# Layer 3's residual sums made by accumulating DMA stores instead of pool engine additions

## The chip, the cores and the metric

The kernel runs on one core of one Trainium2 chip. A core has five engines that run their own instruction streams and wait for each other by semaphores: TensorE (PE, matmuls into PSUM), VectorE (DVE), ScalarE (ACT), the pool engine (GpSimd, POOL) and SyncE (SP), which issues most of the transfers. Transfers run on 16 DMA engines that all issuers share; ScalarE and the pool engine issue some as well. The metric is the device time of the one launch in microseconds (us), as a median of runs.

## What is computed

The reference passes 2048 tokens (2 sequences of 1024) of 256 channels through four layers. Each layer makes a condition `c` from the stream `x` and adds a mixture of experts of that condition to the stream:

```
x = x + _L0_ffn_ref(_L0_cond_ref(x, ...), ...)
x = x + _L1_ffn_ref(_L1_cond_ref(x, ...), ...)
x = x + _L2_ffn_ref(_L2_cond_ref(x, ...), ...)
x = x + _L3_ffn_ref(_L3_cond_ref(x, ...), ...)
```

Layer 3 is where the change lies. Its condition is a shared two-matrix network plus two of eight experts for every token, weighted and divided by 3. Its last part, `_L3_ffn_ref`, sends each token to one of 16 experts, the one with the largest logit. An expert takes at most 160 tokens (the kernel plans 128 rows and 32 more for each), and what it writes for a token *replaces* that token's row:

```
safe_idx = jnp.where(valid, idx, bt)
y_flat = x_flat.at[safe_idx.reshape(-1)].set(out.reshape(-1, d), mode='drop')
```

Here `x_flat` is the condition itself. So the output of a token is `x + c` when it was not taken by an expert, and `x + out` when it was. With `x` the stream ahead of layer 3 and `c` its condition, every row of the output first needs the base value `x + c`, and the rows of taken tokens are then written over.

## The kernel before, in words

The work is tiled by 128 tokens: 16 tiles, in four blocks (`NB`) of 512 tokens (`TB`). The stream lies in the tile `Xt` (token-major, 128 partitions by 16 tiles by 256 channels); the condition of layer 3 is summed in `Ht`, which the profile calls `ACC`, as it lies in that buffer. `HT` and `XT` hold the channel-major copies that matmuls need.

**Layer 3's condition** (`_cond_moe`, called with `next` set to an object of class `Last`). A first phase does the shared network for blocks 0 to 2 (`lead` is 3). After each step of it a hook is called, and the hook advances the routing in the object `Lead`, whose counter `n` counts the calls: four for each block. The routing ends in 32 indirect scatters of `Xt` rows from the pool engine (L282). Then come the experts' slots, 37 of them in most cases: a load of rows, matmuls, and an indirect scatter of the results into the DRAM buffer `tbuf`. Then `next.begin()` prepares the last layer, and a second phase does the shared network for block 3 (`_shared`, matmuls at L1534 and L1520) and, in hooks, the tokens' sums.

**The sums** are in class `Tokens`. For each of the 16 tiles, SP loads the two expert results of each token (`yt`, L298, 256 KB, five buffers), and VectorE adds them with their weights into `ACC` (two instructions at L1665). A tile that is done is turned by TensorE (`ps_bk`, L1588) and copied by ScalarE into `HT` (L1591). Which tiles are due at which hook is a list (`by`).

**The last layer's routing** (`Last.chunk`) is cut into parts for each block of 512 tokens, and these are threaded into the hooks by a written-out plan: first `logits`, then `top`, `rows` and the `beats` that rank the tokens. `logits` is the part that the change edits. It issues from ScalarE a store of the block's condition rows into the left half of a DRAM buffer `hx` (L2217), and on the pool engine an addition of the block's condition into the stream, in place (L2219). Then come matmuls for the logits (`l3f_pt`, L2223). `top` has the small VectorE instructions on `l3f_pl` (L2236 to L2248, with an exponential on ScalarE at L2242); `rows` makes `l3f_z` and TensorE's `l3f_ps` (L2266), and on the pool engine a running count `l3f_cum` (L2271).

**`hx`** holds for each token its condition (left) and the stream ahead of layer 3 (right, one store of the whole `Xt` at L2190 in `begin`). The last layer gathers rows of it by expert (`Last.run`, L338 from the pool engine), computes, adds the right half to the result (L2427), and scatters the sums into the output (L2428, pool engine).

**The base rows** go to the output in `Last.finish`: four stores of 512 KB from SP (L2340), one for each block of `Xt`, after the pool additions. Behind them on SP stand the loads of the biases (`XT<-in_L_b`, L2345; `ACC<-in_L_b`, L2393) and of weights. The scatters into the output wait for these stores by name (`self.outs`).

**Order.** The program is recorded in Python; a scheduler places the instructions on the engines by what is ready, and `_behind` adds an order without a semaphore. A DMA has one of eight completion semaphores for its kind of issuer, in turn; a DMA that takes a semaphore over waits for the one that had it.

Of the kernel before, what the change touches and what calls it, by code (L numbers as in the profile page):

```python
# [15 lines left out]
ALU = mybir.AluOpType  # L16
# [4 lines left out]
P = 128  # L21
D = 256
# [5 lines left out]
TB = 512  # L28
NB = N // TB
# [1459 lines left out]
def _behind(k, inst, ref):  # L1489

    k.tc.add_manual_dep(inst.ins, ref.ins.name,
                        mybir.DependencyInfo(mybir.DependencyClass.NoSync,
                                             mybir.DependencyReason.SCHED_ONLY))
# [433 lines left out]
def _cond_moe(k, name, wr, bias, W1, W3, W2, nf, hold, R1, R2, gate_mult, final, lead, most, next=None):  # L1927

    nc, A, XT, HT, Xt, Ht = k.nc, k.A, k.XT, k.HT, k.Xt, k.Ht
    rp, pool, psum = k.rp, k.pool, k.psum  # L1930
    E, T, NS = 8, P, 39
    base = 0 if next else 8192
    w, rb = k.small[wr], k.small[bias]
    sets = []
    for i in range(4):
        r = k.ring.take(1, hold).rearrange("p (n c f) -> p n c f", n=2, f=D)
        sets.append([(r[:, 0], A[R1]), (r[:, 1], A[R2])])
    def routing(lead_):
        s = rp.tile([P, NT, E], F32, name=name + "_s", tag="s")
        _logits(k, psum, rp, XT, w, E, name, s, AF.Sigmoid, k.small[wr, "b"])  # L1940
        sel = rp.tile([P, NT, E], F32, name=name + "_sel", tag="lg")
        nc.vector.tensor_tensor(sel, s, _bc(rb, 1, [P, NT, E]), ALU.add)
        _, ixf = _top(nc, rp, sel, E, name)
        _name_rows(k, k.Xr, ixf, base)
        oh = [_one_hot(k, rp, ixf, n, E, name + "_oh%d" % n, "oh%d" % n) for n in range(2)]
        M = rp.tile([P, NT, E], F32, name=name + "_M", tag="M")
        nc.vector.tensor_add(M, oh[0], oh[1])
        cum = _running(k, rp, M, E, name)
        yield
        pos, eid, of, used = _route(k, rp, psum, M, cum, E, T, NS, len(sets), name)  # L1950
        rows = [_rows_of(k, rp, oh[n], pos, E, name + "_rows%d" % n, "rows%d" % n) for n in range(2)]
        k.x.begin()
        lead_.sends = k.x.paced(k.Xr, rows)

        nc.vector.tensor_mul(M, M, s)
        den = rp.tile([P, NT], F32, name=name + "_den", tag="den")
        nc.vector.tensor_reduce(den, M, AX.X, ALU.add)
        big = rp.tile([P, NT], F32, name=name + "_big", tag="big")
        nc.vector.tensor_single_scalar(big, den, 1e-9, ALU.is_gt)
        nc.vector.tensor_scalar_add(den, den, 1e-9)  # L1960
        nc.vector.reciprocal(den, den)
        nc.vector.tensor_mul(den, den, big)
        nc.vector.tensor_scalar(big, big, -0.5, 0.5, ALU.mult, ALU.add)
        gate = []
        for n in range(2):
            nc.vector.tensor_mul(oh[n], oh[n], s)
            g = rp.tile([P, NT], F32, name=name + "_g%d" % n, tag="g%d" % n)
            nc.vector.tensor_reduce(g, oh[n], AX.X, ALU.add)
            nc.vector.tensor_mul(g, g, den)
            nc.vector.tensor_add(g, g, big)  # L1970
            nc.vector.tensor_scalar_mul(g, g, gate_mult * final)
            gate.append(g)
        lead_.made = gate, eid, of, used

    def shared(tb, hook=None, mid=None, added=lambda: False):
        if nf == 8 and tb == 0:
            po = _shared_first(k, pool, psum, XT, W1, W3, W2, hook)
        else:
            po = _shared(k, pool, psum, XT, tb, W1, W3, W2, nf, hook, mid)
        for i in range(2):  # L1980
            t = tb * 4 + i * 2
            if added():
                nc.vector.scalar_tensor_tensor(Ht[:, t:t + 2, :], po[i], final, Ht[:, t:t + 2, :],
                                               ALU.mult, ALU.add)
            else:
                nc.scalar.activation(Ht[:, t:t + 2, :], po[i], AF.Copy, scale=final)

    lead_ = Lead(k, routing, *((1, 7), 2) if nf == 8 else ((1, 3), 4))
    def hook(f, mul, mm):
        if k.late and lead_.n >= 6:  # L1990
            k.late.pop(0)(mul)
        lead_.hook(f, mul, mm)

    for tb in range(lead):
        shared(tb, hook)
    gate, eid, of, used = lead_.finish()
    k.t.begin()
    by = Slots(k, pool, psum, of, base)

    def slots(lo, hi):  # L2000
        series = Series(k, by, lo, hi)
        for i in range(lo, hi):
            series.slot(i, _gelu_products(k, pool, psum), lambda: _slot_weights(k, eid, i, sets, E))
        series.close()

    used = nc.values_load(used[0:1, 0:1], min_val=0, max_val=NS)
    slots(0, most)
    with k.tc.If(used > most):  # L2008
        slots(most, NS)
    if next:  # L2010
        next.begin()
    c = Tokens(k, pool, psum, gate, Ht, HT, nf, next)
    for tb in range(lead, NB):
        c.there = tb * 4
        shared(tb, c.hook, c.hook, lambda: c.added >= tb * 4 + 4)
    c.there = NT
    k.ring.drop(hold)
    if next:
        next.finish(c)
    else:  # L2020
        c.finish()
# [104 lines left out]
class Last:  # L2126
# [46 lines left out]
    def begin(self):  # L2173

        k, nc = self.k, self.k.nc
        nc.vector.memset(self.acc, 0.0)
        for t in range(NT):
            c = sum((q + 1) * TB - max(t * P, q * TB) for q in range(t // 4, NB) if self.on_act(t))
            c -= P * sum(self.on_act(u) for u in range(4 * (t // 4) + 4) if u <= t)
            nc.gpsimd.memset(self.acc[:, t, 4:5], float(c))  # L2180
        nc.vector.memset(self.z, 0.0)
        for side, at, v in ((0, self.E, 1.0), (1, self.E, -1.0)):
            nc.vector.memset(self.z[:, :, side, at:at + 1], v)
        for i in range(3):
            nc.vector.memset(self.z[:, :, 0, self.PARTS + 2 * i:self.PARTS + 2 * i + 1], 1.0)
            nc.vector.memset(self.z[:, :, 1, self.PARTS + 2 * i + 1:self.PARTS + 2 * i + 2], -1.0)
        nc.vector.memset(self.cum[:, 0, :], 0.0)
        nc.vector.tensor_scalar(self.down, k.iota[:, 0:self.E], -1.0, float(self.E), ALU.mult, ALU.add)
        nc.vector.tensor_scalar_add(self.th, k.iota[:, 0:NT], 1.0)
        nc.sync.dma_start(k.hx[:, D:2 * D].rearrange("(t p) d -> p t d", p=P), k.Xt)  # L2190
        self.weights()

    def on_act(self, t):

# [11 lines left out]
    def chunk(self, q):  # L2206
        k, nc, E = self.k, self.k.nc, self.E
        pool, psum = k.pool, k.psum
        ts, cols = slice(4 * q, 4 * q + 4), slice(q * TB, (q + 1) * TB)
# [5 lines left out]

        def logits(mul, mm):
            nc.scalar.dma_start(k.hx[cols, 0:D].rearrange("(t p) d -> p t d", p=P), k.Ht[:, ts, :])  # L2217
            x = k.Xt[:, ts, :]
            nc.gpsimd.tensor_tensor(x, x, k.Ht[:, ts, :], ALU.add)  # L2219
            ps = psum.tile([P, P], F32, name="l3f_pt", tag="mm")  # L2220
            for c in range(2):
                for j in range(4):
                    i = nc.tensor.matmul(ps[32 * j:32 * j + 32, :], k.small["L3_Wg"][:, c, :],  # L2223
                                         k.HT[:, c, (4 * q + j) * P:(4 * q + j + 1) * P],
                                         start=c == 0, stop=c == 1, skip_group_check=True)
                    behind(i, mm)
            lt = got["lt"] = pool.tile([P, P], F32, name="l3f_lt")
            nc.scalar.copy(lt, ps)
# [94 lines left out]
    def finish(self, c):  # L2323

        k, nc, E = self.k, self.k.nc, self.E
# [4 lines left out]
        ref = None  # L2330
        for x in todo:
            if callable(x):
                x()
            else:
                for p in x:
                    ref = p(None, None) or ref
        ref = _warm(k, k.psum, ref, 6)
        assert c.put == NT
        for q in range(NB):
            i = nc.sync.dma_start(k.out[q * TB:(q + 1) * TB, :].rearrange("(t p) d -> p t d", p=P),  # L2340
                                  k.Xt[:, 4 * q:4 * q + 4, :])
            _behind(k, i, c.load)
            self.outs.append(i.ins.name)
        for e in range(E):
            i = nc.sync.dma_start(self.b2[:, e, :], k.A["L3_b2"][e:e + 1].to_broadcast([P, D]))  # L2345
            _behind(k, i, c.load)
# [7 lines left out]
        for h in range(4):  # L2354
            A = k.HT[:, 0, 256 * h:256 * h + 256].bitcast(BF16).rearrange("p (t r) -> p t r", r=P)
            ts = slice(4 * h, 4 * h + 4)
            made = nc.vector.tensor_tensor(A, _bc(k.iota16[:, 0:P], 1, [P, 4, P]),  # L2357
                                           _bc(rank16[:, ts], 2, [P, 4, P]), ALU.is_equal)
            for j in range(4):
# [3 lines left out]
                ref = i  # L2363
# [6 lines left out]
        ref = _warm(k, k.psum, ref, 4)  # L2370
        ps = k.psum.tile([P, 2, E], F32, name="l3f_pi2", tag="t", bufs=2)
        for t in range(NT):
# [3 lines left out]
            ref = i  # L2376
# [3 lines left out]
        for g in range(4):  # L2380
# [3 lines left out]
            ref = i  # L2384
        self.ref = ref
        s, d, _ = self.numbers(pg, 4, "g")
# [236 lines left out]
```

## Time and profile before

| what | us |
|---|---|
| median of 3 runs | 1445.5 (1445.5 to 1446.88) |
| the profiled execution | 1446.02 |
| its span, first to last instruction | 1444.3 |
| TensorE busy | 1396.8 (97% of the span) |
| VectorE busy | 464.0 (32%) |
| ScalarE busy | 307.8 (21%) |
| pool engine busy | 291.5 (20%) |
| the four additions at L2219 | 9.7, 2.418 each |

The granted TensorE clock is 0.988 on the mean. A row of a timeline gives the start in us, the duration, the engine, the line, the operation, what it writes and reads, the number of instructions merged into the row, and in brackets how long the engine sat idle ahead of it and what ended that. A row of a group or of a tile's list gives the count and the least, median and greatest duration in ns, and when the first and the last started. A row of busy time by stretch gives the stretch, its length, the busy time of PE, of the weight loads (PEld), DVE, ACT and POOL with the number of instructions, then the granted clock, the mean share in which the 16 DMA engines were busy, and GB/s.

### The profile page before, as it was taken

How to read it: one execution, taken by the hardware profiler on the slowest of the kernel's cores; microseconds unless marked ns; L12 is line 12 of the kernel's file. 1: busy time of each engine (PE TensorE's matmuls, PEld its weight loads, DVE VectorE, ACT ScalarE, POOL GpSimd, SP SyncE). 2: the span in 40 equal slices, each digit the busy share in tenths (PEclk: the TensorE clock that was granted, in tenths of full speed). 3: DMA queues.
4: the chain of work that ended last, by engine and by line, in shares of the span. 5: the costliest groups of instructions: out<-in, count | busy, mean ns of one | idle time of the engine just before them, and what ended most of it. 6: DMA issues, size and time to landing. Idle time of an engine off the chain costs nothing. (4 is left out here: it accounts for less than half of the span.)

```text
span 1444.3 us, 23566 instructions
## 1 busy us (share of the span) xinstructions
PE 1396.8 (97%) x8606; PEld 1002.0 (69%) x8610; DVE 464.0 (32%) x1558; ACT 307.8 (21%) x646; POOL 291.5 (20%) x339
## 2 busy tenths in 40 slices
PE   9999999999999999999999999999999998997897
PEld 4544444545558865565999999999995567874675
DVE  4523322326214442511211111111115513467332
ACT  3222221234112121201111111111112211126221
POOL 0400001200533410331001001001010073433441
PEclk9999999999999999999999999999999999998999
DMA  9879994922314850421335155155507247758470
GB/s 313 297 256 347 358 321 134 275 72 101 125 52 118 260 183 8 188 82 37 113 109 194 48 180 195 46 178 194 193 20 273 93 164 244 225 172 284 123 243 15
DMA packets 176527, 246.78 MB, mean 171 GB/s; under 512 B 16695, under 2 KB 128831, under 8 KB 176400
## 3 DMA queue, kind: packets, MB, share of 16 engines
q1 hardware_dynamic: 154912, 203.18, 43.1%
q0 software_dynamic: 13888, 36.63, 7.2%
q10 hardware_dynamic: 7600, 5.34, 1.1%
q8 instruction: 72, 1.18, 0.3%
q14 instruction: 55, 0.45, 0.1%
HBM read 280.92 MB, written 47.22 MB: 227 GB/s over the span
## 5 line engine op out<-in xcount | busy, mean ns | idle before, releaser
L282 POOL DMA_INDIRECT tbuf<-ys,sdst x108 | 106.3, 984 | 484.8 <-ACT ys L1844 376.6
L1520 PE MATMUL spo<-ring,sa 128*128 128x256 f32 x704 | 164.9, 379 | 0.0
L1520 PEld LDWEIGHTS spo<-ring,sa 128*128 128x128 f32 x704 | 132.5, 190 | 44.6 <-issue 29.1
L1837 DVE TENSOR_TENSOR fa<-fsg,fpu 128x512 f32<-128x512 f32 x72 | 49.5, 688 | 316.2 <-PE fpu L1832 316.2
L1832 PE MATMUL fpg<-xsT,ring 128*128 128x128 f32 x1152 | 140.4, 275 | 0.7 <-issue 0.7
L1543 DVE TENSOR_TENSOR sa<-ssg,spu 128x512 f32<-128x512 f32 x88 | 60.4, 686 | 249.8 <-PE spu L1534 241.2
L1832 PE MATMUL fpu<-xsT,ring 128*128 128x128 f32 x1152 | 140.4, 275 | 0.0
L1832 PEld LDWEIGHTS fpg<-xsT,ring 128*128 128x128 f32 x1152 | 137.0, 192 | 2.7 <-issue 0.9
L1832 PEld LDWEIGHTS fpu<-xsT,ring 128*128 128x128 f32 x1152 | 134.4, 192 | 0.0
L1841 PE MATMUL fpo<-ring,fa 128*128 128x256 f32 x576 | 130.3, 379 | 0.0
L1841 PEld LDWEIGHTS fpo<-ring,fa 128*128 128x128 f32 x576 | 106.7, 190 | 13.0
L1539 ACT ACTIVATE ssg<-spg 128x512 f32<-128x512 f32 x88 | 52.6, 597 | 263.0 <-PE spg L1534 243.6
L1534 PE MATMUL spg<-HT,ring 128*128 128x512 f32 x192 | 92.1, 594 | 2.2 <-issue 1.9
L1534 PE MATMUL spu<-HT,ring 128*128 128x512 f32 x192 | 90.2, 592 | 0.0
L1808 PE MATMUL cph<-xsT,ring 128*128 128x128 f32 x576 | 79.0, 281 | 4.8 <-DMA ring<-in_L_r 2.6
L1836 ACT ACTIVATE fsg<-fpg 128x512 f32<-128x512 f32 x72 | 43.0, 597 | 171.7 <-PE fpg L1832 171.7
L1808 PEld LDWEIGHTS cph<-xsT,ring 128*128 128x128 f32 x576 | 71.2, 194 | 8.8 <-DVE sn L1735 2.8
L1534 PE MATMUL spg<-XT,ring 128*128 128x512 f32 x160 | 75.5, 593 | 1.3 <-PEq L2008 1.2
L1534 PE MATMUL spu<-XT,ring 128*128 128x512 f32 x160 | 75.2, 592 | 0.0
L1815 PE MATMUL cpo<-ring,ch 128*128 128x256 f32 x288 | 73.8, 380 | 0.0
L1534 PEld LDWEIGHTS spu<-HT,ring 128*128 128x128 f32 x192 | 36.3, 190 | 45.0 <-issue 44.2
L1731 DVE COPY xsT<-ps_cm 128x256 f32<-128x256 f32 x132 | 55.1, 418 | 36.7 <-PE ps_cm L365 36.5
(621 smaller groups left out, 1726.1 us busy)
## 6 DMA issues: line engine op xcount, KB each, us to landing
ring<-in_L_w SPq DMA_DIRECT2D x108, 1024.0 KB
ring<-in_L_r SPq DMA_DIRECT2D x72, 512.0 KB
ring<-in_L_r SPq DMA_DIRECT2D x144, 256.0 KB
xs<-xbuf SPq DMA_DIRECT2D x132, 129.0 KB
ring<-in_L_W SPq DMA_DIRECT2D x32, 512.0 KB
yt<-tbuf SPq DMA_DIRECT2D x48, 256.0 KB
XT<-in_L_r SPq DMA_DIRECT2D x16, 512.0 KB
HT<-in_L_r SPq DMA_DIRECT2D x8, 512.0 KB
```

Source lines behind the costliest of these rows:

```text
L282: i = k.nc.gpsimd.indirect_dma_start(out=self.ap, out_offset=bass.IndirectOffsetOnAxis(ap=idx, axis=0), in_=rows, in_offset=None, **end)
L1520: mm = nc.tensor.matmul(po[g // 2][:, g % 2, :], a[:, g * P:(g + 1) * P], W2[:, f, :], start=f == 0 and g % 2 == 0, stop=f == nf - 1, skip ...
L1534: mm = nc.tensor.matmul(ps, W[:, c, f * P:(f + 1) * P], X[:, c, cols], start=c == 0, stop=c == 1)
L1539: k.silu = nc.scalar.activation(sg, pg, AF.Silu)
L1543: mul = nc.vector.tensor_mul(a, sg, pu)
L1731: turned = nc.vector.tensor_copy(xT, _channel_major(k, self.psum, xs, made=made))
L1808: made = [nc.tensor.matmul(ph[:, f, :], R1[:, c, f * P:(f + 1) * P], xT[:, c, :], start=c == 0, stop=c == 1) for f in range(2) for c in ra ...
L1815: made = [nc.tensor.matmul(po, h[:, f, :], R2[:, f, :], start=f == 0, stop=f == 1) for f in range(2)]
L1832: made = [nc.tensor.matmul(ps[:, j, :], W[:, c, (f0 + j) * P:(f0 + j + 1) * P], xT[:, c, :], start=c == 0, stop=c == 1) for ps, W in ((pg, ...
L1836: nc.scalar.activation(sg, pg, AF.Silu)
L1837: nc.vector.tensor_mul(a[:, f0:f0 + 4, :], sg, pu)
L1841: made = [nc.tensor.matmul(po, a[:, f, :], W2[:, f, :], start=f == 0, stop=f == 4 * nh - 1) for f in range(4 * nh)]
```

## The change

The store of the whole `Xt` to the right half of `hx` moves out of `begin` into a new method `base`, which also stores `Xt` to the output. `base` is called from the hook of the first phase, at the fourth call. In `logits` the pool engine's addition is replaced by a DMA that the pool engine issues, which adds the block's condition rows onto the rows in the output. The four stores of finished sums in `finish` go. So `Xt` keeps the stream ahead of layer 3 to the end.

```diff
@@ _cond_moe, hook
         lead_.hook(f, mul, mm)
+        if next and lead_.n == 4:
+            next.base(mul)
@@ Last.begin
-        nc.sync.dma_start(k.hx[:, D:2 * D].rearrange("(t p) d -> p t d", p=P), k.Xt)
         self.weights()
+
+    def base(self, ref):
+
+        for to in (self.k.hx[:, D:2 * D], self.k.out):
+            i = self.k.nc.sync.dma_start(to.rearrange("(t p) d -> p t d", p=P), self.k.Xt)
+            if ref is not None:
+                _behind(self.k, i, ref)
@@ Last.chunk, logits
-            x = k.Xt[:, ts, :]
-            nc.gpsimd.tensor_tensor(x, x, k.Ht[:, ts, :], ALU.add)
+            i = nc.gpsimd.dma_start(k.out[cols, :].rearrange("(t p) d -> p t d", p=P), k.Ht[:, ts, :],
+                                    accum_op=ALU.add)
+            self.outs.append(i.ins.name)
@@ Last.finish
-        for q in range(NB):
-            i = nc.sync.dma_start(k.out[q * TB:(q + 1) * TB, :].rearrange("(t p) d -> p t d", p=P),
-                                  k.Xt[:, 4 * q:4 * q + 4, :])
-            _behind(k, i, c.load)
-            self.outs.append(i.ins.name)
```

## The prediction

> **What bounds the kernel now.** I read the page's busy shares first: TensorE is busy 97% of the span, so most of the kernel can't be touched by an edit on the pool engine. I then went to the chain that ended last, in order of time, and looked where it leaves TensorE. From 1283 to 1343 us it runs over VectorE (the adds of layer 3's condition into `ACC`, then the routing of the last layer). So I read this stretch engine by engine. The pool engine's timeline there has the four additions that the change removes:
>
> ```profile
> 1288.46 2.48 POOL L2219 TENSOR_TENSOR Xt<-Xt,ACC 128x1024 f32<-128x1024 f32 x1 [8.40 <-issue]
> 1294.34 2.48 POOL L2219 TENSOR_TENSOR Xt<-Xt,ACC 128x1024 f32<-128x1024 f32 x1 [3.40 <-DVE ACC L1665]
> 1300.22 2.35 POOL L2219 TENSOR_TENSOR Xt<-Xt,ACC 128x1024 f32<-128x1024 f32 x1 [3.40 <-DVE l3f_m L2236]
> ...
> 1309.32 2.36 POOL L2219 TENSOR_TENSOR Xt<-Xt,ACC 128x1024 f32<-128x1024 f32 x1 [3.90 <-DVE l3f_lg L2238]
> ```
>
> Beside them, VectorE's instructions on the tile `yt`, and its timeline:
>
> ```profile
> L1665 DVE SCALAR_TENSOR_TENSOR ACC<-yt,l3c_g,ACC x32: 470/474/2596, 1284.0 to 1308.7; 128x256 f32<-128x256 f32 x32
> ```
>
> ```profile
> 1286.43 5.59 DVE L1665 SCALAR_TENSOR_TENSOR ACC<-yt,l3c_g,ACC 128x256 f32<-128x256 f32 x8
> 1291.94 0.68 DVE L1543 TENSOR_TENSOR sa<-ssg,spu 128x512 f32<-128x512 f32 x1
> 1292.54 5.36 DVE L1665 SCALAR_TENSOR_TENSOR ACC<-yt,l3c_g,ACC 128x256 f32<-128x256 f32 x8
> ...
> 1300.25 0.23 DVE L2238 TENSOR_TENSOR l3f_lg<-l3f_pl,l3f_m 128x64 f32<-128x64 f32 x1
> 1300.51 2.12 DVE L2241 TENSOR_SCALAR l3f_eq<-l3f_lg 128x64 f32<-128x64 f32 x1
> 1302.66 0.22 DVE L2243 TENSOR_TENSOR l3f_eq<-l3f_eq,l3f_down 128x64 f32<-128x64 f32 x1
> ```
>
> An add at L1665 takes 474 ns, but two take about 2590, and those two start inside the first two pool additions and end as they end. The third addition catches `l3f_eq`: 2.12 us, where the same instruction takes 0.19 at 1312.28. So each of three additions stops VectorE: 2.12 + 2.11 + 1.93 = 6.2 us. The fourth falls into a VectorE wait for TensorE (2.37 us, to 1311.66).
>
> Is that on the path? TensorE's timeline answers:
>
> ```profile
> 1298.46 0.60 PE L1588 MATMUL ps_bk<-ident,ACC 128*128 128x128 f32 x4
> 1298.90 0.27 PE L2232 MATMUL l3f_pl<-ident,l3f_lt 128*128 128x128 f32 x1
> 1299.01 1.89 PE L1520 MATMUL spo<-ring,sa 128*128 128x256 f32 x8
> 1301.02 0.72 PE L1588 MATMUL ps_bk<-ident,ACC 128*128 128x128 f32 x4
> 1303.23 0.71 PE L1588 MATMUL ps_bk<-ident,ACC 128*128 128x128 f32 x4 [1.50 <-ACT HT L1591]
> 1305.52 0.62 PE L2266 MATMUL l3f_ps<-ident,l3f_z 128*128 128x128 bf16 x8 [1.57 <-DVE l3f_z L2260]
> ```
>
> Until 1301 TensorE has no idle; from there it waits for ScalarE and VectorE. The first two stalls lie beside a full TensorE, the third lies where TensorE waits.
>
> **The change part by part.** Working against the profiled execution (1446.02 us, span 1444.3; 0.52 above the median 1445.5).
>
> *Base rows to the output, early.* The 2 MB store of `Xt` to `hx` is issued at 1125.90 and its traffic is over by 1135; the order of instructions has the new 2 MB store to `out` right behind it on SP, with a wait only for a load of 1119. SP issues nothing more until 1153.96, as it waits for `l3c_used`; the DMA share is 0.61 from 1126 to 1136 and 0.00 from 1135 to 1150. So the second store (some 9.5 us if it runs like the first alone) is covered: 0. If it were not over by 1152.88, it would meet the scatters of layer 3, whose last one TensorE awaits for 4.86 us at 1192.
>
> *The four output stores at L2340 go.* They are behind all `yt` loads on SP; SP gets to the bias loads (1303.10) and weights (1317.19) 3 to 5 us earlier. No piece of the chain waits for those: 0. The stores' 2 MB leave the stretch 1300 to 1315, where the DMA share is 0.79 to 1.09.
>
> *Four pool additions go: the first two.* After the first stall, VectorE is 2.1 us earlier at `sa` (1291.94). Without the second it would reach the last `sa` at 1293.6, but `spu` ends only at 1295.7, so it waits. From there: `sa` 0.6, four adds 1.67, so tile 11 is done by 1298.05 instead of 1300.0; `l3f_m` then waits for `l3f_pl`, which ends at 1299.17 on the full TensorE. `l3f_m` starts at about 1299.2 instead of 1300.0: 0.8 us of 4.2 is kept.
>
> *The third.* `l3f_eq` saves 1.93. What is late next is ScalarE: its table load before the exponential (1.28 us at 1301.26) follows two copies that follow tile 11; it can end at 1300.95 instead of 1302.54, 0.35 after VectorE would want it. So 1.93 - 0.35 = 1.6, and `l3f_ps` starts at 1303.1 instead of 1305.52: **2.4 us** in all.
>
> *The clock.* TensorE's granted clock is 1.00 up to 1306.8, 0.50 from there to 1310.2, and 1.00 again; this follows the stretch with two idle gaps of 1.5 us. These rows of busy time by stretch have the clock ahead of the last two columns:
>
> ```profile
> 1300.00:1303.42 3.42, 1.81 (x11) 1.04 (x9) 3.23 (x7) 2.69 (x7) 2.35 (x1) 1.00 0.85 265
> 1303.42:1306.83 3.41, 1.84 (x28) 1.47 (x31) 3.23 (x14) 2.38 (x7) 1.78 (x6) 1.00 1.09 384
> 1306.83:1310.24 3.41, 3.41 (x34) 2.03 (x29) 2.08 (x8) 1.36 (x5) 0.92 (x1) 0.52 0.87 256
> ```
>
> With work moved 2.4 us earlier, 1303.42 to 1306.83 holds near 3 us of TensorE work, so I take it that the clock stays. Four transposes then take 0.60 as at 1298.46, not the 1.12 of 1307.17; followed through `l3f_pl`, the last add and `l3f_lt` (0.27 at 1310.71) this is 0.8 us, bounded by 0 (the clock falls anyway) and 1.7 (half of the 3.4).
>
> *Four accumulating stores are added.* No row of before shows one. On the pool engine: the row nearest in kind is a scatter of 128 rows (0.96 us, and 0.30 to the next); a 512-row store is bounded by one (0.96) and four of them (4 x 1.26 = 5.0). I take 2.5, about an addition's length. Queued behind the third is `l3f_cum`, which now would be due at 1300.9; the store starts by 1298.3, so 2.5 costs nothing and 5.0 costs 0.7 (TensorE wants `l3f_cum` at 1303.6, it takes 2.0). VectorE ran with 4.84 us of 5 busy from 1150 to 1155 while scatters were issued in 1.04 and 0.96 us, and none of its instructions there lasted 2 us, so I count no stall on either side.
>
> The Trainium skill speaks against this in "SBUF — State Buffer", section "SBUF: two separate sides": while VectorE runs in a mode that takes both its ports, the pool engine can't write the descriptors of its DMAs. By that, issues would stretch beside VectorE; the 0.96 us rows don't show it.
>
> On the DMA engines: from below, 512 KB at the pace of the lone `hx` store (2 MB in 9.5 us) is 2.4 us; from above, four scatters end to end, at 3.1 us to landing, are 12.4. I take the lower, as the row nearest in shape. From 1285 to 1300 the share is 0.89, so 1.65 us are free. Two accumulating stores fall there, 4.8 us. The last `yt` load is issued at tile 10, about 1297.2, and used at 1305.4; the first load took 2.8 from issue to use, so there are 5.4 us of slack: 0 at the lower price. What waits for these stores by order (the gathers from 1343, the group bias loads from 1325) has over 15 us.
>
> The skill's "Collectives: The Full Stack", section "The bandwidth ceiling", says that an add in the DMA engines reads two sources through one ring, at half a copy's rate. By that each store costs an estimated 4.8, which no run here shows; 9.6 less 1.65 and 5.4 makes the loads 2.6 us late, and the sum would be -0.6 instead of the one below.
>
> **Sum:** -2.4 - 0.8 = -3.2: 1446.02 - 3.2 = 1442.8 for the profiled execution, **1442.3** against the median. From there to 1343 the chain is made of short steps that all follow, and the last layer's slots move as one.
>
> **Rivals.**
> *Accumulating stores starve the loads (slower).* At 12.4 us each, taking half of the engines' turns, two hold 12.4 us; less 1.65 free and 5.4 slack, the sums are 5.4 late, less the 2.4 gained: +3.0. Taking all turns, 24.8 gives +15.4. So 1448.5 to 1461. It decides from about 9.5 us held by the two. For: the engines are at 0.89 and more, and the adds are fed five buffers deep. Against: the slack.
> *ScalarE is held.* Its last `hx` store now waits on a semaphore last used by the tenth bias load; in before that load was issued at 1312.16, now at some 1306 to 1308, landing about 2.8 later; ScalarE wants to go on at 1307.5 to 1308.4. With that or a clock that falls anyway, 0.5 to 2.4 is left: 1443.1 to 1445.
> *All stalls pay.* If TensorE's order gives way to the earlier sums or a later half-clock stretch (1317, 1324) goes too: -4.2 to -6.2, 1439.3 to 1441.3.
> *It doesn't do what it says.* If issuing the store stops VectorE as the addition did, nothing changes: 1445.5.
>
> **How the numbers follow.** Forecast 0.42, all stalls 0.12, ScalarE or clock 0.14, starving 0.28, no effect 0.04. 0.2% is 2.9 us, about what a measurement of this kernel can tell from no change. Faster: 0.36 of the forecast's (its low side keeps under 2.9) and 0.12, 0.48. Slower: 0.26. Within: the rest, 0.26. The range goes from 1439.5, nearly all of the best case, to 1452, the cheaper third of the starving case; some 0.18 is left out, nearly all above.
>
> **What would show it.** In the profile after: no L1665 above 0.5 us and `l3f_eq` at 0.2; `l3f_ps` 2.4 us earlier against the first `yt` add; clock 1.00 in the stretch after it; POOL rows for the stores under 3 us; no VectorE wait for `yt` beyond the first. It is wrong if L1665 waits for `yt` from 1288 on, if ScalarE sits before its last `hx` store, or if the first gather doesn't move.

## The result, and the profile after

The changed kernel is slower: 1453.54 us (1448.88 to 1458.16, 16 runs) against 1447.34 (1445.5 to 1451.92, 16 runs) beside it, a ratio of 1.0041 (95% interval 1.0029 to 1.0052). The forecast was 1442.3 and faster, worked from a median of three runs, 1445.5; the time lies above the range. The profiled execution took 1456.02 us (span 1454.3), 2.5 over its median. In it the first `yt` add comes at 1285.97, 1.98 later than in the profile of before, an offset made earlier in the kernel (with the runs below the first add comes anywhere from 1293.0 to 1300.1); so positions are given from that add, and line numbers up to L1990 are as they were, later ones 2 to 9 higher.

The pool engine's timeline has the four stores where the additions were, and they are short:

```profile
1290.79 1.42 POOL L2226 DMA_DIRECT2D out<-ACC  x1 [8.75 <-DVE ACC L1665]
1295.16 1.30 POOL L2226 DMA_DIRECT2D out<-ACC  x1 [2.96 <-DVE ACC L1665]
1303.17 1.27 POOL L2226 DMA_DIRECT2D out<-ACC  x1 [6.70 <-issue]
...
1312.24 1.33 POOL L2226 DMA_DIRECT2D out<-ACC  x1 [6.03 <-ACT HT L1591]
```

VectorE's instructions on `yt`, and its timeline in the same stretch:

```profile
L1665 DVE SCALAR_TENSOR_TENSOR ACC<-yt,l3c_g,ACC x32: 473/477/486, 1286.0 to 1311.2; 128x256 f32<-128x256 f32 x32
```

```profile
1288.41 2.13 DVE L1665 SCALAR_TENSOR_TENSOR ACC<-yt,l3c_g,ACC 128x256 f32<-128x256 f32 x5
1291.15 1.27 DVE L1665 SCALAR_TENSOR_TENSOR ACC<-yt,l3c_g,ACC 128x256 f32<-128x256 f32 x3 [0.61 <-DMA yt<-tbuf]
...
1297.68 1.28 DVE L1665 SCALAR_TENSOR_TENSOR ACC<-yt,l3c_g,ACC 128x256 f32<-128x256 f32 x3 [2.68 <-DMA yt<-tbuf]
...
1301.35 1.27 DVE L1665 SCALAR_TENSOR_TENSOR ACC<-yt,l3c_g,ACC 128x256 f32<-128x256 f32 x3 [1.40 <-DMA yt<-tbuf]
...
1303.05 0.20 DVE L2250 TENSOR_SCALAR l3f_eq<-l3f_lg 128x64 f32<-128x64 f32 x1
...
1304.06 0.43 DVE L2264 CAST l3f_z<-l3f_oh 128x128 bf16<-128x128 f32 x1
```

No add lasts 2.59 us any more and `l3f_eq` takes 0.20: all three stalls are gone. A small one is new: the cast of 1304.06 takes 0.43 us, where its other three take 0.23 to 0.28, and ends 0.05 us after the issue of the third store. VectorE's next instruction waits 0.88 us for ScalarE, so no time is seen to be lost by it. What costs are three new brackets: VectorE now waits 0.61 + 2.68 + 1.40 = 4.7 us for `yt`. So `l3f_ps`, 21.53 us after the first add before, is at 21.23, 0.3 earlier and not 2.4:

```profile
1307.20 0.72 PE L2275 MATMUL l3f_ps<-ident,l3f_z 128*128 128x128 bf16 x8 [0.84 <-DVE l3f_z L2269]
```

The busy time by stretch shows why the loads are late: the DMA share (the column before the last) is 1.11 to 1.19, and the half clock still begins near 1308:

```profile
1300.00:1304.00 4.00, 3.33 (x20) 2.59 (x18) 2.48 (x9) 0.86 (x3) 0.83 (x1) 1.00 1.15 294
1304.00:1308.00 4.00, 1.77 (x16) 1.23 (x15) 2.92 (x13) 3.69 (x9) 1.99 (x7) 0.95 1.11 326
1308.00:1312.00 4.00, 4.00 (x41) 2.77 (x44) 2.59 (x9) 1.77 (x5) 0.00 (x0) 0.63 1.19 245
```

The loss itself comes after that, in ScalarE's timeline:

```profile
1312.43 0.27 ACT L2237 COPY l3f_lt<-l3f_pt 128x128 f32<-128x128 f32 x1
1320.76 0.37 ACTq L2225 DMA_DIRECT2D hx<-ACC  x1
1321.16 0.37 ACT L1591 COPY HT<-ps_bk 128x256 f32<-128x256 f32 x1 [8.47 <-DMA XT<-in_L_b]
```

In the profile of before, the same store and copy:

```profile
1310.81 0.37 ACTq L2217 DMA_DIRECT2D hx<-ACC  x1
1311.88 0.37 ACT L1591 COPY HT<-ps_bk 128x256 f32<-128x256 f32 x1 [0.91 <-PE ps_bk L1588]
```

ScalarE does nothing for 8.5 us, with its last `hx` store at the end of that time; in the profile of before it stood 0.91 us there. The chain that ended last, in this stretch (start, us, what), says what it waited for:

```profile
1301.35 1.27 DVE ACC L1665 x3
...
1302.66 10.72 DMA hx<-ACC
...
1313.83 0.43 SPq L2349
...
1314.31 6.35 DMA XT<-in_L_b
...
1320.76 0.37 ACTq L2225
...
1321.16 0.38 ACT HT L1591
```

Read it upwards. The last `hx` store takes over the semaphore of the tenth bias load, so it waits for that load. That load stood on SP behind the eighth, which takes over the semaphore of the third `hx` store, and this store took 10.7 us to land. The semaphore numbers in the traces agree: the eighth bias load is the next transfer on the third `hx` store's semaphore (106), and the last `hx` store the next on the tenth bias load's (108). In the trace of before, the last `hx` store takes 108 over from the third output store, issued 8.2 us ahead of it. The first gather is at 66.20 instead of 59.20: 7.0 us late. From there to the last scatter nothing much differs (94.65 us, 93.97 before).

### The profile page after: what moved, and what is told of

It reads as the page before. It is cut to its first block, busy times and chain, and to the rows that moved or that the text cites. A ratio compares the mean times of both kernels' runs of the same rounds, so it can differ in the third digit from the quotient of the medians.

```text
span 1454.3 us, 23560 instructions
## 1 busy us (share of the span) xinstructions
PE 1400.5 (96%) x8606; PEld 1005.0 (69%) x8610; DVE 458.2 (32%) x1558; ACT 307.6 (21%) x646; POOL 286.9 (20%) x339
```

## The experiments

Two theories. **L**: the chain of semaphores through ScalarE's last `hx` store is the loss. **D**: the accumulating stores' time on the DMA engines is: it makes `yt` late, and it makes the third `hx` store late, without which the chain would hold nobody. A third, **B**, has the early store of the base rows as the cost.

The runs are on other chips, where the kernel before takes 1457 to 1458.4 us, so the ratio to the kernel before on the same chip is what counts. Each of e1 to e16 has 5 to 12 runs. The other columns are from one profile each, which can lie up to 4.5 us off the median of its runs: VectorE's waits for `yt` after the first, then, from the first `yt` add, `l3f_ps` and the first gather, and from that gather its first use (`l3f_ph`) and the last scatter.

| run | ratio to before (95%) | `yt` waits | `l3f_ps` | first gather | `l3f_ph` | last scatter |
|---|---|---|---|---|---|---|
| before | 1 | 0 | 21.5 | 59.2 | 4.6 | 94.0 |
| after | 1.0041 (1.0029 to 1.0052) | 4.7 | 21.2 | 66.2 | 4.8 | 94.7 |
| e1 no stores | 0.9967 (0.9955 to 0.9980) | 1.2 | 19.2 | 55.0 | 4.7 | 94.6 |
| e2 plain stores | 0.9980 (0.9967 to 0.9992) | 3.3 | 19.7 | 57.2 | 4.6 | 94.6 |
| e3 bias loads behind | 1.0003 (0.9990 to 1.0015) | 5.5 | 22.3 | 61.1 | 4.7 | 94.0 |
| e4 stores late | 1.0010 (0.9996 to 1.0023) | 1.6 | 19.2 | 56.7 | 4.8 | 97.3 |
| e5 after again | 1.0049 (1.0036 to 1.0062) | 3.9 | 20.8 | 65.7 | 4.8 | 94.4 |
| e6 late, bias behind | 1.0008 (0.9995 to 1.0021) | 4.2 | 20.8 | 59.9 | 5.1 | 99.8 |
| e7 stores mid | 0.9990 (0.9976 to 1.0003) | 1.3 | 19.0 | 52.9 | 5.5 | 95.4 |
| e8 no stores, no base | 0.9978 (0.9968 to 0.9988) | 1.3 | 19.0 | 56.0 | 4.6 | 94.2 |
| e9 last hx from pool | 1.0001 (0.9988 to 1.0014) | 4.5 | 21.1 | 59.4 | 4.8 | 94.4 |
| e10 before, weights last | 1.0005 (0.9996 to 1.0014) | 0.4 | 21.8 | 60.4 | 4.6 | 94.1 |
| e11 mid, weights last | 1.0000 (0.9989 to 1.0011) | 2.9 | 19.4 | 54.2 | 7.5 | 97.7 |
| e12 top, weights last | 1.0000 (0.9990 to 1.0009) | 1.8 | 19.0 | 55.5 | 7.7 | 97.6 |
| e13 mid, weights wait | 0.9970 (0.9957 to 0.9983) | 4.0 | 20.7 | 58.9 | 4.7 | 94.6 |
| e14 top, weights wait | 0.9957 (0.9940 to 0.9974) | 2.2 | 19.4 | 57.2 | 4.7 | 94.0 |
| e15 before, weights wait | 0.9997 (0.9983 to 1.0011) | 0 | 21.3 | 59.4 | 4.6 | 94.7 |
| e16 no stores, wait | 0.9960 (0.9946 to 0.9974) | 2.6 | 19.3 | 56.5 | 4.6 | 94.0 |

### What the stores cost in all, and which part is the addition

e1 takes the stores out of `logits`; e2 takes only `accum_op=ALU.add` out of them.

```diff
-            i = nc.gpsimd.dma_start(k.out[cols, :]..., k.Ht[:, ts, :], accum_op=ALU.add)
-            self.outs.append(i.ins.name)
```

> Leaves out the four accumulating stores; nothing takes their place, so the output holds the stream without the condition's rows. The order of the loads and stores on SP and ScalarE, and which of them share a semaphore, stay as in the changed kernel. Theory L (a chain of shared semaphores alone: third hx store, eighth bias load, tenth bias load, ScalarE's last hx store): the third hx store then lands in 3 to 4 us instead of 10.7, so most of the 8.5 us before ScalarE's copy goes too, and the time is some 1442 to 1444. Theory D (the accumulating stores' time on the DMA engines is the cause of both that wait and of VectorE's 4.7 us for yt): the same here, 1441 to 1443, with no VectorE wait for yt after the first. Theory B (the early store of the base rows, or the loads that come earlier since the four output stores went, is what costs): the time stays within 2 us of the changed kernel's 1453.5.

> The same four stores from the pool engine, at the same places, without the addition: the output's rows are the condition alone. If the price is that of 2 MB more to be written (any store would do it), the time is within 1 us of the changed kernel and VectorE still waits 4 to 5 us for yt. If it is the addition in the DMA engines, the stores take about half the DMA time, the third hx store lands in 4 to 6 us, and the time is 1442 to 1447.

Without the stores the kernel is 0.33% (4.8 us) faster than before; on the scale of the kernel before at 1447.34 that is 1442.6, as L and D both have it. B falls here: the early base store is still in e1. D also had no wait for `yt` here, and 1.2 us of it stay. SP waits 0.3 us for an `hx` store where it waited 7.2. `l3f_ps` is 2.4 us earlier, just what the sum of the prediction had; its first add is at 1300.08, and `l3f_m` waits for TensorE as that sum has it:

```profile
1315.43 0.23 DVE L2242 TENSOR_REDUCE l3f_m<-l3f_pl 128x4 f32<-128x64 f32 x1 [1.14 <-PE l3f_pl L2238]
```

The plain stores keep most of that: 1444.4 on the same scale, which was expected if the addition in the DMA engines is the price. The DMA queues say what the addition costs. The columns are packets, MB, and the share of 16 engines' time; first the accumulating stores in the profile after, 1288 to 1326, then the plain ones in e2, 1298 to 1325:

```profile
q0 software_dynamic: 2112, 2.10, 37.2%
```

```profile
q0 software_dynamic: 576, 2.10, 20.9%
```

37.2% of 38 us is 14.1 us of all engines, 3.5 for each store, and 20.9% of 27 is 5.6, 1.4 for each: for the same bytes the adding store takes 2.5 times the DMA time. Its median time from issue to landing is 11.6 us.

### The semaphore alone

e3 orders the sixteen bias loads behind ScalarE's last `hx` store; e9 leaves SP's order and issues that one store from the pool engine. e5 is the changed kernel again.

```diff
             i = nc.sync.dma_start(self.b2[:, e, :], k.A["L3_b2"][e:e + 1].to_broadcast([P, D]))
             _behind(k, i, c.load)
+            _behind(k, i, self.sent)
```

```diff
-            nc.scalar.dma_start(k.hx[cols, 0:D]...
+            (nc.gpsimd if q == NB - 1 else nc.scalar).dma_start(k.hx[cols, 0:D]...
```

> The changed kernel with the sixteen bias loads placed behind ScalarE's last hx store, so that the load whose semaphore that store takes over is the last yt load. Theory L: ScalarE's 8.5 us wait goes, the first gather is about 7 us earlier, and the time is 1446 to 1448 (the 4.7 us that VectorE waits for yt stay). Theory D in its narrow form (only the late yt loads and the clock count): 1452 to 1454, as ScalarE then waits for something else.

> The changed kernel with one edit: the last of the four hx stores is issued by the pool engine and not by ScalarE, so no instruction of ScalarE stands behind a store that takes a bias load's semaphore over; the order of loads on SP stays. Theory L: ScalarE's copy of tile 15 follows its transpose at once, the first gather comes at 60 to 62 us after the first yt add (66 with the changed kernel, 59.2 before), and the time is 0 to 0.1% over the kernel before, as with the bias loads moved. If what the moved bias loads cured was traffic and not the semaphore, this stays 0.4 to 0.5% over.

> The changed kernel once more, on the chip of this group, so that the next three stand beside it. Both theories: 0.3 to 0.5% slower than the kernel before, first gather 7 us later against the first yt add (66.2 us against 59.2), and ScalarE's wait of about 8 us before its last hx store again. If that wait is not there, it was an accident of one execution, and the ratio of 1.0041 needs another reason.

ScalarE's copy, e3 and then e9:

```profile
1324.75 0.37 ACTq L2225 DMA_DIRECT2D hx<-ACC  x1
1325.83 0.37 ACT L1591 COPY HT<-ps_bk 128x256 f32<-128x256 f32 x1 [0.91 <-PE ps_bk L1588]
```

```profile
1324.18 0.37 ACT L1591 COPY HT<-ps_bk 128x256 f32<-128x256 f32 x1 [0.91 <-PE ps_bk L1588]
```

Both are back at the 0.91 us of before, while e5 stands 7.86 us there. Two different edits give the same answer: 1.0003 and 1.0001, where the changed kernel has 1.0041 and, again, 1.0049. So the hold is worth 0.4 to 0.5%, some 6 us, and L is shown. What is left against e1, 0.35% or 5 us, is what the stores cost without the hold. D's account of it fits: `yt` waits of 4.5 to 5.5 us where e1 has 1.2, and `l3f_ps` 2 to 3 us later. The hold needs both: in e1 the semaphores are the same, and ScalarE's copy isn't late (24.9 us after the first add, 27.9 before).

### The early base store

e8 is e1 without the second store in `base`.

> No accumulating stores and no early store of the base rows to the output (the store to the right half of hx stays): rows that no expert takes are left unwritten. Both theories, and the step that priced the early store at nothing: the same time as without the accumulating stores alone, 0.33% under the kernel before, within 0.1%. If the early store costs something, 0.4% or more under the kernel before.

0.9978 against 0.9967, 0.11% apart where 0.1 was allowed, with intervals that overlap: no cost is seen, and if anything this kernel, which does less, is the slower. The trace after agrees: the DMA share is 0.74 from 1126 to 1136, 0.49 to 1146 and 0.00 to 1153.

### Moving the stores out of the sums

In e4 they stand in `finish`, behind the routing; e6 has that and e3's edit; in e7 all four stand right behind the last `hx` store, and the bias and weight loads are ordered behind them.

```diff
+            if q == NB - 1:
+                for b in range(NB):
+                    i = self.sent = nc.gpsimd.dma_start(
+                        k.out[b * TB:(b + 1) * TB, :].rearrange("(t p) d -> p t d", p=P),
+                        k.Ht[:, 4 * b:4 * b + 4, :], accum_op=ALU.add)
+                    _behind(k, i, hx)
+                    self.outs.append(i.ins.name)
```

> The four accumulating stores moved behind the last layer's routing, into the matmuls that keep TensorE warm; semaphores on SP and ScalarE as in the changed kernel. Theories L and D: the sums run undisturbed as without the stores; the stores' 46 us of landing at 11.6 each, if they run one beside the other, fall between 1322 and 1345, where the weight loads run: 1442 to 1446, the upper end if the weight loads or the first gathers come late. Theory B: 1452 to 1454.

> Both cures together: the accumulating stores behind the routing, and the bias loads behind ScalarE's last hx store. Theory L and D added up: without the stores' load in the sums and without the shared semaphore, the first gather comes some 4 us earlier than in the kernel before against the first yt add, as without the stores, and the time is 0.2 to 0.35% under the kernel before, if the stores' own DMA time is over before the gathers; 0 to 0.1% over it, if the tail that the late stores showed (2.7 us later from the first gather to the last scatter) is theirs and not the clock's.

> All four accumulating stores right behind ScalarE's last hx store, with the bias loads and weight loads behind them. Theory D: the last yt load has landed by then, so VectorE doesn't wait for yt, ScalarE isn't held, and the stores' 14 us of all DMA engines (four at 3.5) plus the 6 MB of weights and biases are over by about 52 us after the first yt add, 5 before the gathers: 0.2 to 0.35% under the kernel before. If the accumulating stores hurt by more than DMA time (the pool engine's issue beside VectorE's counting, some 5 us of it), the time is that of the kernel before or over it.

e4 and e7 miss; e6 lands where it was expected if the tail from the first gather on is the stores' (0 to 0.1% over), and its tail is 99.8 us. All undo the loss, but none gains what e1 gains. In e4 and e7 the sums run as without the stores, and the first gather is 2.5 and 6.3 us earlier than before; then 3.3 and 1.4 us are given back by the last scatter. e6's profile is 4 us over its median, and its `yt` waits of 4.2 us, with no such store near, aren't explained by D. Left open by these three: DMA time, or something else of the stores?

### The weight loads in the way of the gathers

e11 and e12 record the last eight weight loads (512 KB each) behind the first gathers. e11 has e7's stores; e12 has the bias loads first and the stores behind the last block's softmax sums (`top`). e10 is the kernel before with the same move.

> A control: the kernel before, with its last weight loads (eight of 512 KB) moved from behind the bias loads to behind the first gathers. Both theories: the stretch from 1317 to 1343 has DMA time free in the kernel before, so nothing is gained there: within 0.1% of the kernel before; over it if the weights come late for the last experts.

> The accumulating stores right behind ScalarE's last hx store and the bias loads behind them, as in the earlier run that came to 0.1% under the kernel before, and the weight loads behind the first gathers. Theory D (only the DMA engines' time counts, 14 us for the four stores): with 4 MB less to move before the gathers the stores end some 10 us before them, and the time comes to that without the stores, 0.25 to 0.35% under the kernel before. If they still cost something there (the pool engine's issue beside VectorE, a clock that falls at another place), it stays at 0.1% under.

> As the run beside it, but the bias loads come first, right behind the last hx store, and the accumulating stores some 6 us later, behind the last block's softmax sums, so that the hx store lands undisturbed and SP doesn't stand 12 us at a semaphore that it holds. Theory D: 0.25 to 0.35% under the kernel before, the same as the run beside it or 0.05% better. If the stores' issue (5 us of the pool engine) holds back the running counts of the last blocks, which are on the pool engine too, the first gather comes 2 to 4 us later than in the run beside it.

e10 is as expected. e11 and e12 miss what D had, but the profile shows why. TensorE's first work on a gathered tile, in e11:

```profile
1348.90 1.11 POOL L338 DMA_INDIRECT HT<-hx,l3f_src  x1 [18.20 <-DVE l3f_i L2412]
...
1355.18 0.69 PE L365 MATMUL ps_cm<-ident,HT 128*128 128x128 f32 x2 [4.44 <-DMA HT<-hx,l3f_src]
```

From the gather's issue to the matmul 6.3 us pass (3.5 in e1). The order that was recorded doesn't hold back SP at run time: it has nothing to wait for but the semaphores that its loads take over, and issues the eight weight loads from 1340.92 to 1346.06, 8.0 to 2.8 us ahead of the gather. So e13, e14 and e15 are e11, e12 and e10 with a semaphore: the weight loads wait for VectorE's copy of the fifth gathered tile. e16 is e1 with it.

```diff
-            nc.vector.tensor_copy(xT, _channel_major(k, psum, at[i], self.ref))
+            turned = nc.vector.tensor_copy(xT, _channel_major(k, psum, at[i], self.ref))
+            if n == 4:
+                self.weights(wait=turned)
```

> The accumulating stores right behind ScalarE's last hx store, the bias loads behind them, and the last eight weight loads made to wait (by a semaphore) for VectorE's copy of the fifth gathered tile. In the run without that wait the weight loads started 4 to 8 us ahead of the first gather and the first matmul of the last layer came 7.5 us after it, where 4.6 to 4.8 is usual. Theory D: with the wait that is 4.6 to 4.8 again, and the time is 0.2 to 0.3% under the kernel before. If the stores cost something that is no DMA time, it stays at 0 to 0.1% under.

> The same wait of the weight loads, with the bias loads first and the accumulating stores behind the last block's softmax sums. Theory D: 0.2 to 0.3% under the kernel before, first matmul of the last layer 4.6 to 4.8 us after the first gather.

> A control: the kernel before with the weight loads made to wait for the copy of the fifth gathered tile, and nothing else changed. If the gain of the two runs ahead of it is that of the additions that went, this one is within 0.1% of the kernel before; if it is the wait's own (gathers that meet no weight loads), this one gains 0.1 to 0.3% too.

> The bound from below: no accumulating stores at all (the output holds the stream without the condition's rows), weight loads waiting as in the three runs ahead of it. Theory D: 0.3% under the kernel before, and the two kernels with the stores come within 0.1% of it. If they stay 0.2% or more behind it, the stores still cost something where the DMA engines are free.

The same rows in e14:

```profile
1352.83 1.10 POOL L338 DMA_INDIRECT HT<-hx,l3f_src  x1 [19.70 <-DMA ACC<-in_L_b]
...
1356.32 0.69 PE L365 MATMUL ps_cm<-ident,HT 128*128 128x128 f32 x2 [1.66 <-DMA HT<-hx,l3f_src]
```

3.5 us again. e14 is at 0.9957 and e13 at 0.9970, level with e16's 0.9960, which has no stores; the wait alone (e15) gives nothing. For e14 the 0.2 to 0.3% expected are at the low end of its interval. So the stores cost DMA time and nothing else that these runs can tell, and where that time is free they cost nothing, to within the runs' 0.15% or so (2 us). The profile of e13 can't show this: its execution took 4.5 us more than the median, and its `yt` waits of 4.0 us stay open as e6's do. **e14 beats both kernels**: 1452.32 us (6 runs) beside 1458.4 for the kernel before, 0.43% (0.26 to 0.60). Its four stores, with little beside them, from 1325.6 to 1341.6:

```profile
q0 software_dynamic: 2101, 2.09, 89.2%
q1 hardware_dynamic: 740, 0.67, 14.8%
```

89.2% of 16 us is 14.3 us of all engines, as in the profile after: the price doesn't come from the crowd.

## Why the prediction was wrong, step by step

The sum was -2.4 - 0.8 = -3.2, with the accumulating stores at 0 and ScalarE's hold outside it. The runs have -4.8 without the stores (e1), some +5 for the stores alone (e3 and e9 against e1) and some +6 for the hold (the changed kernel against e3 and e9): +6.2 in all.

- **Stalls of the additions** (-2.4 us, and all of the three gone): right, and by the way that was worked out. e1 has `l3f_ps` 2.4 us earlier, and its `l3f_m`, 15.35 us after the first add, waits for `l3f_pl` as the sum had it (15.2).
- **The clock** (-0.8): not seen in the changed kernel, whose half clock came 21.6 us after the first add, where it came at 23.0 before. In e1 and e7 the clock is 1.00 until 24 us after the first add, where before it was 0.87 from 20 to 24; but the half clock only comes later there, at 27.3 and 27.8. The whole gain without stores is 4.8 us (2.9 to 6.6) where the sum had 3.2. How much of the rest is the clock wasn't separated.
- **The early base store** and **the stores that went** (0 each): the first is right by trace and e8. The second ("No piece of the chain waits for those: 0") overlooked what stood behind those stores: all sixteen bias loads, and not seven, now come ahead of the last `hx` store in the order in which semaphores are handed out, and the transfer eight places ahead of it is the tenth of them.
- **The pool engine's share** (2.5 taken, 0.96 to 5.0): 1.27 to 1.42 us each, so the bounds held. "I count no stall on either side" is nearly right: no add is stretched, but the cast beside the third store's issue is, by 0.2 us, and in e3, e5 and e9 as well. The Trainium skill's rule in "SBUF — State Buffer", section "SBUF: two separate sides", that the pool engine can't write descriptors while VectorE runs in a mode that takes both its ports, isn't seen in these issues, which stay at 1.27 to 1.42 us; here it was VectorE that took longer.
- **The DMA price** (2.4 taken, up to 12.4): wrong. 3.5 us of all engines for each store, 2.5 times a plain one. I took the plain store as the nearest row in shape and so left out the addition; and 2.4 was the elapsed time of a lone store that had the engines at 0.61, so 1.5 us of all of them, near e2's 1.4. The Trainium skill's "Collectives: The Full Stack", section "The bandwidth ceiling", has an add in a collective at half a copy's rate; its ratio of 2 is near the 2.5 measured. The sum by it (-0.6) was nearer the truth than mine, but it had no hold either.
- **"5.4 us of slack: 0 at the lower price"**: wrong in a second way. Only the last load's slack was worked out, and VectorE waits at earlier ones, from 1291 on. `yt` waits of 1.2 to 4.2 us stand even in the runs with no accumulating store near, probably since VectorE, without its stalls, catches up with its loads; that was not tested. With the stores they are 3.9 to 5.5.
- **The rival "ScalarE is held"**: the mechanism that decided, named in the prediction, and **the step that failed is its price**: "in before that load was issued at 1312.16, now at some 1306 to 1308, landing about 2.8 later". I followed that load's issue on SP but not SP's own wait, two loads ahead, for the semaphore of the third `hx` store, and gave that store no delay from the accumulating ones. It was issued at 1314.3 and landed 6.4 us later, and the hold cost some 6 us, not a part of the gain.
- **The rival "starve the loads"**, from 9.5 us held by two: two hold 7.1, under its point, and the `yt` waits alone (e3, e9) only cancel the gain (1.0003 and 1.0001). The two rivals were priced apart; the loss needed both, as the stores' DMA time is what made the hold long.

## What to carry to other kernels

Price a DMA that adds by a row that adds, or, without one, well over a plain store (2.5 times in DMA time here), and then ask which transfers are in flight beside it and who takes over *their* semaphores. When DMAs are removed or added, write out the order in which the shared semaphores are handed out: an engine that must issue a transfer in order can come to wait for a load it has no use for. An order that is only recorded doesn't hold a transfer back at run time; where a load must stay out of the way, it needs a wait.

## What the runs showed of the hardware that was not expected

- An accumulating store of 512 KB moved packets of about 1 KB (2112 for four stores and 2 MB), where the plain stores from the same engine and tile had 576; it held the 16 DMA engines for 3.5 us against 1.4, and landed after 11.6 us beside other traffic.
- The DMA share goes over 1 while the bytes fall: 1.24 at 198 GB/s beside the accumulating stores in e14, 1.06 at some 370 under weight loads. A low GB/s is no sign of free engines.
- Some of VectorE's small instructions last longer beside the pool engine's issue of a store. The cast `l3f_z` took 0.43 us for 0.23 in the changed kernel, e3, e5 and e9, and ended 0.05 us after the issue each time; in e12 and e14 `l3f_eq` took 0.52 for 0.19. The adds at L1665 took their 0.48.
- A run's profile may lie 4 us from the median of its runs (e6, e13, e14), about as much as the effects here; the first gather against the first add holds better (66.2 and 65.7 for the changed kernel, 59.2 and 59.4 in the profile of before and e15).
